# The end of a spectral ffn: the last back-transform with two places side by side in the two halves of the array

## The chip, the cores and the metric

The kernel runs on one core of a Trainium2 chip. The metric is the device time of one execution in microseconds, as the median of several runs. All data are fp32.

## What is computed

The reference is two layers on `x` of shape (2, 128, 64, 64). The first is a convolutional neighbourhood attention block, the second full attention over the 4096 tokens of each image, followed by a spectral ffn. Only the end of the ffn bears on the change:

```python
U_plus  = irfft(rfft(phi) * rfft(u))             # 16 filters, causal convolution over t
U_minus = sgn * irfft(rfft(phi) * rfft(u * sgn)) # the same with alternating signs
out = einsum('btkd,k,kde->bte', U_plus, s, Mpp) + einsum('btkd,k,kde->bte', U_minus, s, Mpm)
out = out + sum(shift(u, i) @ Mu[i] for i in range(3))
t = t + weighted sum of out over four branches (prefixes of 1, 1/2, 1/4 and 1/8 of the tokens)
x = from_tokens(t)                               # back to (2, 128, 64, 64)
```

The convolution is done by transforms of blocks of the tokens into a frequency domain of 160 bins (`BINS`), with real and imaginary parts as 320 rows (`NC`), products there, a projection from channels to channels in each bin, and a transform back, whose result is added to `t`.

## The kernel before

The kernel is one long program. In the last part, the tokens of an image lie in `xa[b]`, 128 channels by 4096 tokens, ordered by parity `par`, half `h`, block `f` (8 of them, `FB`) and place within a block `c`. Adding the transformed result there finishes the work; what then remains is to write the output.

The bins are handled in 40 groups of four (`GB`). A group consists of filter products (`group`, L1304, whose results ACT and DVE copy into `y` at L1305) and of the projection (`project`, L1316), 32 products that add up in one PSUM tile `acc`. ACT moves each `acc` into the tile `ob` (L1322), which holds channels by (parity, image, block, bin, real or imaginary part). The order of TensorE's work in this loop is written out by hand (`tc.manual_schedule`).

The back-transform takes the bins in three chunks: 0 to 63, 64 to 127 and 128 to 159, the last with 32 bins and so 64 rows only. For each image, parity and pair of blocks, `turn` brings the bins onto the partitions by transposes on TensorE (L1332), and ACT copies the result into `t` (L1334). `back` multiplies by the table `inv` (L1343). The first two chunks are woven into the loop as `back_into`, two blocks at a time, and DVE adds the result into `xa` (L1355). The table `inv` holds three parts of 128 rows; `_transforms` fills 320 of these rows, and the last 64 are zero.

The third chunk needs the last group and comes after the loop, in 16 rounds of four blocks:

```python
last = [(h, b, par, f0) for h in range(2) for b in range(NB) for par in range(2) for f0 in range(0, FB, 4)]
```

A round transposes four blocks one at a time, each to 64 rows (L1332), copies them (L1334), multiplies each by 128 columns of `inv` (L1343), and lets DVE add the result and `xa` into the output tile `o` (L1391). The transposes of a round are issued one round ahead. The same blocks are transposed twice, once for each half `h` of the tokens. After four rounds `o` is complete, and SP issues its transfer of 1 MB to the output (L1395). `o` has two buffers, `t` has two. PSUM has eight banks here: two for `acc`, and six in the pool `ps_c` with the tag `pc`, which `pc`, `pt` and `py` share in turn.

In the profile, L1332, L1334, L1343 and L1391 after 2207 us are this end.

Of the kernel before, what the change touches and what calls it, by code (L numbers as in the profile page):

```python
# [8 lines left out]
F32 = mybir.dt.float32  # L9
AF = mybir.ActivationFunctionType  # L10
ALU = mybir.AluOpType
# [3 lines left out]
P = 128  # L15
NB = 2
T = 4096
TH = T // 2
# [62 lines left out]
CB, FB, SG = 256, 8, 4  # L81
SB = CB // SG
NC = CB + SB

CHUNKS = (0, 1, 4, 5, 2, 3, 6, 7)
BINS = NC // 2
GB = 4
LG = 2 * FB
GROW = 4 * LG * KF


@with_exitstack
def kernel(
# [16 lines left out]
    nc = tc.nc  # L110
# [12 lines left out]
    xa = [xp.tile([P, T], F32, tag=f"xa{b}", name=f"xa{b}") for b in range(NB)]  # L123
# [15 lines left out]
    ident = const.tile([P, P], F32, name="ident")  # L139
# [79 lines left out]
    with l0a:  # L219
# [64 lines left out]
        for r in range(QT):  # L284
            lo = 6 - min(r, 6)
            src = bass.AP(
                rpb_pad.tensor, (RPR + r - 6) * RPW + 50, [[1, QT], [RPW, (HEADS - 1) * RPR - r // 7], [1, NTAB]]
            )
            rows_ = rev[r * QT : (r + 1) * QT].rearrange("p h n m -> p (h n) m")
# [483 lines left out]
        for k, (b, g) in enumerate(order):  # L773
            t = {}
# [499 lines left out]
    with ExitStack() as cv:  # L1274
        cp = cv.enter_context(tc.tile_pool(name="conv", bufs=5))
        obp = cv.enter_context(tc.tile_pool(name="ob", bufs=1))
        ps_c = cv.enter_context(tc.tile_pool(name="ps_c", bufs=6, space=PSUM))
        ps_p = cv.enter_context(tc.tile_pool(name="ps_p", bufs=2, space=PSUM))

        ob = obp.tile([P, 2, NB, FB, BINS, 2], F32, name="ob")  # L1280

        def inputs(q):

            ut = cp.tile([P, NB, 2, P], F32, tag="ut", name="ut")
            nc.sync.dma_start(
                out=ut.rearrange("p b s d -> p (b s d)"),
                in_=us[2 * q : 2 * q + 2].rearrange("g i r f b s d -> (g i r f) (b s d)"),
            )
            return ut

        def group():


            y = cp.tile([P, 8, KF, 2, 32], F32, tag="y", name="y", bufs=2)
            for q in range(GB // 2):
                ct, ut = ahead.pop(0)
                for par in range(2):

                    cv_ = ct[:, :, 0 : 288 + par * 32].rearrange("p o (l c) -> p o l c", l=2)[:, :, :, 0 : FB * KF]
                    for b in range(NB):  # L1300
                        for f in range(2):
                            fp = slice(f * 64, (f + 1) * 64)
                            pc = ps_c.tile([P, 2, 2, FB * KF], F32, tag="pc", name="pc")
                            nc.tensor.matmul(pc, lhsT=ut[fp, b, par, :], rhs=cv_[fp], start=True, stop=True)  # L1304
                            (nc.scalar.copy if f else nc.vector.tensor_copy)(  # L1305
                                y[:, 4 * f : 4 * f + 4, :, par, b * 2 * FB + q : (b + 1) * 2 * FB : 2],
                                pc.rearrange("p r l (t k) -> p (r l) k t", k=KF),
                            )
                if to_load:
                    q_ = to_load.pop(0)  # L1310
                    ahead.append((blocks(q_), inputs(q_)))
            return y

        def project(g, y, acc, l, k):

            nc.tensor.matmul(  # L1316
                acc, lhsT=(mmi if l else mpl)[:, k, :], rhs=y[:, 1::2, k, ::-1, :] if l else y[:, 0::2, k, :, :],
                start=(l == 0 and k == 0), stop=(l == 1 and k == KF - 1),
            )
            if l == 1 and k == KF - 1:  # L1320
                ov = ob.rearrange("p s b t g r -> p (s b t) (g r)")[:, :, g * GB * 2 : (g + 1) * GB * 2]
                nc.scalar.copy(  # L1322
                    ov.rearrange("p m (q x) -> p x m q", q=2), acc.rearrange("p (x m q) -> p x m q", x=4, q=2)
                )

        def turn(chunk, b, par, f0, n):

            bn = min(64, BINS - chunk * 64)
            pt = ps_c.tile([P, n, P], F32, tag="pc", name="pt")
            for j in range(n):  # L1330
                src = ob[:, par, b, FB - 1 - f0 - j, chunk * 64 : chunk * 64 + bn, :]
                nc.tensor.transpose(pt[0 : 2 * bn, j, :], src.rearrange("p g r -> p (g r)"), ident)  # L1332
            t = cp.tile([P, 4, P], F32, tag="t", name="t", bufs=2)
            nc.scalar.copy(t[0 : 2 * bn, 0:n, :], pt[0 : 2 * bn])  # L1334
            return t

        def back(chunk, t, n, h):

            bn = min(64, BINS - chunk * 64)
            c0, cn = (0, CB) if h is None else (h * P, P)  # L1340
            py = ps_c.tile([P, n, cn], F32, tag="pc", name="py")
            for j in range(n):
                nc.tensor.matmul(  # L1343
                    py[:, j, :], lhsT=t[0 : 2 * bn, j, :], rhs=inv[0 : 2 * bn, chunk, c0 : c0 + cn],
                    start=True, stop=True,
                )
            return py

        def back_into(chunk, b, par, f0):

            t = turn(chunk, b, par, f0, 2)
            yield True
            py = back(chunk, t, 2, None)
            xv = xa[b][:, par * TH : (par + 1) * TH].rearrange("p (h f c) -> p f h c", h=2, f=FB)[:, f0 : f0 + 2]
            nc.vector.tensor_tensor(xv, py.rearrange("p f (h c) -> p f h c", h=2), xv, ALU.add)  # L1355
            yield None

        places = [(b, par, f0) for b in range(NB) for par in range(2) for f0 in range(0, FB, 2)]
        to_load = list(range(BINS // 2))
        ahead = [(ct, inputs(to_load.pop(0))) for ct in first_blocks]  # L1360
        rest = []
        with tc.manual_schedule(engines={mybir.EngineType.PE}):
            y = group()
            for g in range(BINS // GB):
                following = group() if g + 1 < BINS // GB else None
                acc = ps_p.tile([P, 64 * GB], F32, tag="acc", name="acc")
                for l in range(2):
                    for k in range(KF):
                        project(g, y, acc, l, k)
                        if rest and k in ((3, 11) if g >= 128 // GB else (7,)):  # L1370
                            if next(rest[0], None) is None:
                                rest.pop(0)
                y = following
                if (g + 1) * GB in (64, 128):
                    rest += [back_into(g * GB // 64, *p) for p in places]
            for steps in rest:
                for _ in steps:
                    pass


        last = [(h, b, par, f0) for h in range(2) for b in range(NB) for par in range(2) for f0 in range(0, FB, 4)]
        ahead = [turn(2, *last[0][1:], 4)]
        for i, (h, b, par, f0) in enumerate(last):
            if i + 1 < len(last):
                ahead.append(turn(2, *last[i + 1][1:], 4))
            if par == 0 and f0 == 0:
                o = cp.tile([P, P, FB, 2], F32, tag="o", name="o", bufs=2)
            xv = xa[b][:, par * TH + h * (TH // 2) : par * TH + (h + 1) * (TH // 2)]
            xv = xv.rearrange("p (f c) -> p c f", f=FB)
            py = back(2, ahead.pop(0), 4, h)  # L1390
            nc.vector.tensor_tensor(  # L1391
                o[:, :, f0 : f0 + 4, par], py.rearrange("p f c -> p c f"), xv[:, :, f0 : f0 + 4], ALU.add
            )
            if par == 1 and f0 + 4 == FB:
                nc.sync.dma_start(out=outf[b, :, h * TH : (h + 1) * TH], in_=o.rearrange("p c f r -> p (c f r)"))  # L1395


# [19 lines left out]
def _transforms():  # L1417


    import numpy as np  # L1420

    f = np.arange(BINS)[None, :]
    real = (f == 0)

    def parts(n):
        n = np.arange(n)[:, None]
        a = 2 * np.pi * ((f * n) % NC) / NC
        return np.cos(a), -np.sin(a), (1.0 - 2.0 * (n % 2)) + 0.0 * f

    def pack(*cols):  # L1430
        return np.stack(cols, axis=-1).reshape(cols[0].shape[0], -1).astype(np.float32)

    c, m, alt = parts(CB)
    seg = pack(c, np.where(real, alt, m))
    filters = pack(c, np.where(real, 0.0, m), np.where(real, 0.0, -m), np.where(real, alt, c))
    back = np.zeros((3 * P, CB), np.float32)
    back[0:NC] = pack(np.where(real, 1.0, 2.0 * c) / NC, np.where(real, alt, 2.0 * m) / NC).T
    return seg, filters, back


# [49 lines left out]
```

## Time and profile before

| | |
|---|---|
| median of three runs | 2242.7 us (2241.91 to 2243.04) |
| the profiled execution | 2241.68 us |
| its span | 2240.0 us, 31648 instructions |
| TensorE (PE) busy | 2174.1 us, 97% |
| weight loads (PEld) busy | 1344.1 us, 60% |
| VectorE (DVE) busy | 940.5 us, 42% |
| ScalarE (ACT) busy | 780.6 us, 35% |
| GpSimd (POOL) busy | 276.2 us, 12% |
| granted TensorE clock, mean | 0.991 |

Times in the lines are from the start of the span. A line of groups names the source line, the engine, the operation, the written and read tiles, for TensorE its active rows and columns (`64*128`), the shape, and how often (x). Then come the busy time in us, the mean length of one in ns, and the idle time of the engine just before, with what ended it. In a timeline a line has the start, the length, the engine and the group, and in brackets the idle time before it. An fp32 product of TensorE leaves two records, a transpose one. Records of TensorE overlap, because one is still running out while the next streams in; the step from start to start is therefore shorter than the length of one.

### The profile page before, as it was taken

How to read it: one execution, taken by the hardware profiler on the slowest of the kernel's cores; microseconds unless marked ns; L12 is line 12 of the kernel's file. 1: busy time of each engine (PE TensorE's matmuls, PEld its weight loads, DVE VectorE, ACT ScalarE, POOL GpSimd, SP SyncE). 2: the span in 40 equal slices, each digit the busy share in tenths (PEclk: the TensorE clock that was granted, in tenths of full speed). 3: DMA queues.
4: the chain of work that ended last, by engine and by line, in shares of the span. 5: the costliest groups of instructions: out<-in, count | busy, mean ns of one | idle time of the engine just before them, and what ended most of it. 6: DMA issues, size and time to landing. Idle time of an engine off the chain costs nothing.

```text
span 2240.0 us, 31648 instructions
## 1 busy us (share of the span) xinstructions
PE 2174.1 (97%) x11888; PEld 1344.1 (60%) x11888; DVE 940.5 (42%) x3046; ACT 780.6 (35%) x1908; POOL 276.2 (12%) x353
## 2 busy tenths in 40 slices
PE   5899998999999999999999999999999999999998
PEld 3677765544454444544544447767677676767677
DVE  4799985434443346433333351222222323232323
ACT  2889883222332223222222332222322323232322
POOL 3377874200000000000000000000000000000000
PEclk8999998999999999999999999999999999999999
DMA  4222212011000016100000132212212122221101
GB/s 119 65 62 60 62 53 51 1 66 52 24 24 24 19 41 175 33 24 23 2 24 24 47 94 55 59 44 54 59 42 56 45 53 50 49 52 46 43 7 76
DMA packets 174810, 109.53 MB, mean 49 GB/s; under 512 B 26049, under 2 KB 159809, under 8 KB 174146
## 3 DMA queue, kind: packets, MB, share of 16 engines
q1 hardware_dynamic: 171818, 105.24, 18.0%
q10 hardware_dynamic: 2840, 2.27, 0.4%
q8 instruction: 94, 1.54, 0.3%
q14 instruction: 58, 0.48, 0.1%
HBM read 72.87 MB, written 34.60 MB: 48 GB/s over the span
## 4 chain that ended last, share of the span: by engine, by line
PE 86%; DVE 6%; POOL 3%; DMA 2%; ACT 1%; SPq 1%; issue 1%; DVEq 0%; ACTq 0%; POOLq 0%
PE acc L1316 25%; PE pc L1304 13%; PE bank L897 10%; PE own L925 10%; PE other L950 8%; PE bank L911 4%; PE py L1343 2%; PE bank L331 2%; PE bank L188 2%; PE bank L1042 2%; PE bank L1010 1%; PE bank L541 1%; DMA st<-in_m_minus_dram 1%; PE bank L505 1%; PE po L563 1%
## 5 line engine op out<-in xcount | busy, mean ns | idle before, releaser
L1305 DVE COPY y<-pc 128x512 f32<-128x512 f32 x320 | 221.4, 692 | 351.6 <-PE pc L1304 347.9
L904 ACT ACTIVATE e<-bank 128x512 f32<-128x512 f32 x288 | 171.8, 597 | 549.9 <-PE bank L897 415.2
L897 PE MATMUL bank<-cm 128*128 128x512 f32 x576 | 299.7, 605 | 1.4 <-DVE y L652 1.4
L1316 PE MATMUL acc<-y,mpl 128*128 128x256 f32 x1280 | 292.1, 382 | 0.0
L1316 PE MATMUL acc<-y,mmi 128*128 128x256 f32 x1280 | 288.0, 379 | 0.0
L1304 PE MATMUL pc<-ct,ut 64*128 64x512 f32 x1280 | 285.2, 595 | 0.9 <-issue 0.9
L1316 PEld LDWEIGHTS acc<-y,mpl 128*128 128x128 f32 x1280 | 238.2, 190 | 59.3 <-issue 29.6
L1316 PEld LDWEIGHTS acc<-y,mmi 128*128 128x128 f32 x1280 | 242.6, 190 | 32.6
L1305 ACT COPY y<-pc 128x512 f32<-128x512 f32 x320 | 204.5, 639 | 87.3 <-PE pc L1304 87.3
L925 PE MATMUL own<-et,tok 128*128 128x512 f32 x448 | 227.0, 593 | 1.9 <-DVE part L914 1.9
L950 PE MATMUL other<-e,tok 128*128 128x512 f32 x448 | 228.6, 592 | 0.0
L914 DVE CUSTOM_DVE_ANT_0 et<-bank,one 128x512 f32<-128x512 f32 x224 | 145.6, 687 | 166.0 <-PE bank L911 165.9
L1304 PEld LDWEIGHTS pc<-ct,ut 64*128 64x128 f32 x1280 | 121.5, 187 | 145.8 <-issue 140.6
L1322 ACT COPY ob<-acc 128x256 f32<-128x256 f32 x40 | 23.8, 595 | 431.2 <-PE acc L1316 431.2
L925 PEld LDWEIGHTS own<-et,tok 128*128 128x128 f32 x448 | 84.5, 190 | 109.8 <-issue 71.8
L950 PEld LDWEIGHTS other<-e,tok 128*128 128x128 f32 x448 | 85.1, 190 | 106.6 <-issue 105.7
L897 PEld LDWEIGHTS bank<-cm 128*128 128x128 f32 x576 | 96.2, 194 | 74.9 <-issue 46.1
L1355 DVE TENSOR_TENSOR xa<-py,xa 128x512 f32<-128x512 f32 x32 | 22.1, 691 | 281.4 <-PE py L1343 281.4
L911 PEld LDWEIGHTS bank<-ident,e 128*128 128x128 f32 x896 | 102.9, 141 | 56.5 <-issue 42.1
L160 POOL TENSOR_TENSOR ln_rs<-ln_rs,mhalf 128x4 f32<-128x4 f32 x24 | 24.3, 1011 | 848.0 <-DVE ln_rs L159 848.0
L528 ACT ACTIVATE p<-p,mn 128x196 f32<-128x196 f32 x256 | 114.4, 449 | 20.8 <-DVE mn L518 13.4
L911 PE MATMUL bank<-ident,e 128*128 128x128 f32 x896 | 117.3, 274 | 0.0
(199 smaller groups left out, 2311.1 us busy)
## 6 DMA issues: line engine op xcount, KB each, us to landing
ut<-us SPq DMA_DIRECT2D x80, 256.0 KB
us<-ub SPq DMA_DIRECT2D x64, 256.0 KB
vw<-vd SPq DMA_DIRECT2D x256, 49.0 KB
ct<-gs SPq DMA_DIRECT2D x160, 72.0 KB
ct<-gs SPq DMA_DIRECT2D x160, 64.0 KB
gs<-sum SPq DMA_DIRECT2D x20, 256.0 KB
vd<-v SPq DMA_DIRECT2D x128, 32.0 KB
st<-in_m_plus_dram SPq DMA_DIRECT2D x16, 256.0 KB
```

What stands on the lines that cost most here:

```text
L188: nc.tensor.transpose(ps[:, j * P : (j + 1) * P], src[:, j, :], ident)
L331: nc.tensor.matmul(pl, lhsT=wg[:, lo : lo + P], rhs=zT, start=True, stop=True)
L528: nc.scalar.activation(p, p, AF.Exp, bias=t[name + "mn"][:, h : h + 1], scale=-1.0, accum_out=t["den"][:, u, h : h + 1],)
L897: nc.tensor.matmul(ps, lhsT=cm[b][:, n * P : (n + 1) * P], rhs=cm[b][:, chunk(c)], start=True, stop=True)
L904: nc.scalar.activation(e, ps, AF.Exp, bias=0.0, scale=ASCALE, accum_out=part[:, n, c : c + 1])
L911: nc.tensor.transpose(pt[:, k * P : (k + 1) * P], es[k][:, m * P : (m + 1) * P], ident)
L914: nc.vector.tensor_tensor_reduce(et, pt, one, 1.0, 0.0, ALU.mult, ALU.add, part[:, n, a : a + 1])
L925: nc.tensor.matmul(own, lhsT=tok[b][:, n, :], rhs=e, start=first, stop=last)
L950: nc.tensor.matmul(other, lhsT=tok[b][:, 4 * CHUNKS[a] + j, :], rhs=es[j], start=(j == 0), stop=(j == 3))
L1304: nc.tensor.matmul(pc, lhsT=ut[fp, b, par, :], rhs=cv_[fp], start=True, stop=True)
L1305: (nc.scalar.copy if f else nc.vector.tensor_copy)(y[:, 4 * f : 4 * f + 4, :, par, b * 2 * FB + q : (b + 1) * 2 * FB : 2], pc.rearrange("p ...
L1316: nc.tensor.matmul(acc, lhsT=(mmi if l else mpl)[:, k, :], rhs=y[:, 1::2, k, ::-1, :] if l else y[:, 0::2, k, :, :], start=(l == 0 and k = ...
```

## The change

The last chunk gets a tile of its own, `ob_last`, in place of the end of `ob`. `turn` and `back` go; `back_into` holds their code for full chunks, and `t` has four buffers in place of two.

After the loop, 16 transposes take two neighbouring blocks at a time: 2 x 64 rows, the odd block on partitions 0 to 63 and the even one on 64 to 127. Each of the four combinations of image and parity has four of them in one PSUM bank, which ACT copies into `t`; these four tiles are kept for both halves `h`.

Then there are eight rounds, one for each half, image and parity. A round first multiplies the even blocks of `xa` by the identity into the bank `even`. Then come eight products of 64 rows, by turns from partitions 0 to 63 into the bank `odd` and from 64 to 127 onto `even`. ACT copies `even` to the even blocks of `o`, and DVE adds `odd` and `xa` into the odd ones. After two rounds the transfer of `o` is issued, as before. So that `inv` has the last bins on both halves of the partitions, its last 64 rows repeat the 64 before them.

```diff
+BC = 64
...
-        ob = obp.tile([P, 2, NB, FB, BINS, 2], F32, name="ob")
+        ob = obp.tile([P, 2, NB, FB, 2 * BC, 2], F32, name="ob")
+        ob_last = obp.tile([P, 2, NB, FB, BINS - 2 * BC, 2], F32, name="ob_last")
...
             if l == 1 and k == KF - 1:
-                ov = ob.rearrange("p s b t g r -> p (s b t) (g r)")[:, :, g * GB * 2 : (g + 1) * GB * 2]
+                o_, g0 = (ob, g * GB) if g * GB < 2 * BC else (ob_last, g * GB - 2 * BC)
+                ov = o_.rearrange("p s b t g r -> p (s b t) (g r)")[:, :, g0 * 2 : (g0 + GB) * 2]
...
         def back_into(chunk, b, par, f0):
 
-            t = turn(chunk, b, par, f0, 2)
+            pt = ps_c.tile([P, 2, P], F32, tag="pc", name="pt")
+            for j in range(2):
+                src = ob[:, par, b, FB - 1 - f0 - j, chunk * BC : (chunk + 1) * BC, :]
+                nc.tensor.transpose(pt[:, j, :], src.rearrange("p g r -> p (g r)"), ident)
+            t = cp.tile([P, 4, P], F32, tag="t", name="t", bufs=4)
+            nc.scalar.copy(t[:, 0:2, :], pt)
             yield True
-            py = back(chunk, t, 2, None)
+            py = ps_c.tile([P, 2, CB], F32, tag="pc", name="py")
+            for j in range(2):
+                nc.tensor.matmul(py[:, j, :], lhsT=t[:, j, :], rhs=inv[:, chunk, :], start=True, stop=True)
...
-        last = [(h, b, par, f0) for h in range(2) for b in range(NB) for par in range(2) for f0 in range(0, FB, 4)]
-        ahead = [turn(2, *last[0][1:], 4)]
-        for i, (h, b, par, f0) in enumerate(last):
-            if i + 1 < len(last):
-                ahead.append(turn(2, *last[i + 1][1:], 4))
-            if par == 0 and f0 == 0:
+        turned_ = {}
+        for b in range(NB):
+            for par in range(2):
+                pt = ps_c.tile([P, 4, P], F32, tag="pc", name="pt")
+                for i in range(4):
+                    src = ob_last[:, par, b, 2 * i : 2 * i + 2]
+                    nc.tensor.transpose(pt[:, 3 - i, :], src.rearrange("p m g r -> p (m g r)"), ident)
+                turned_[b, par] = cp.tile([P, 4, P], F32, tag="t", name="t", bufs=4)
+                nc.scalar.copy(turned_[b, par], pt)
+        for h in range(2):
+            for b in range(NB):
                 o = cp.tile([P, P, FB, 2], F32, tag="o", name="o", bufs=2)
-            xv = xa[b][:, par * TH + h * (TH // 2) : par * TH + (h + 1) * (TH // 2)]
-            xv = xv.rearrange("p (f c) -> p c f", f=FB)
-            py = back(2, ahead.pop(0), 4, h)
-            nc.vector.tensor_tensor(
-                o[:, :, f0 : f0 + 4, par], py.rearrange("p f c -> p c f"), xv[:, :, f0 : f0 + 4], ALU.add
-            )
-            if par == 1 and f0 + 4 == FB:
+                for par in range(2):
+                    xv = xa[b][:, par * TH + h * (TH // 2) : par * TH + (h + 1) * (TH // 2)]
+                    xv = xv.rearrange("p (f c) -> p f c", f=FB)
+                    odd, even = (ps_c.tile([P, 4, P], F32, tag="pc", name="py") for _ in range(2))
+                    nc.tensor.matmul(even, lhsT=ident, rhs=xv[:, 0::2], start=True, stop=False)
+                    for i in range(4):
+                        for q, py in ((0, odd), (1, even)):
+                            rows_ = slice(q * 64, (q + 1) * 64)
+                            nc.tensor.matmul(
+                                py[:, i, :], lhsT=turned_[b, par][rows_, i, :], rhs=inv[rows_, 2, h * P : (h + 1) * P],
+                                start=(q == 0), stop=(q == 0 or i == 3),
+                            )
+                    nc.scalar.copy(o[:, :, 0::2, par], even.rearrange("p f c -> p c f"))
+                    nc.vector.tensor_tensor(
+                        o[:, :, 1::2, par], odd.rearrange("p f c -> p c f"), xv[:, 1::2].rearrange("p f c -> p c f"), ALU.add
+                    )
                 nc.sync.dma_start(out=outf[b, :, h * TH : (h + 1) * TH], in_=o.rearrange("p c f r -> p (c f r)"))
...
     back[0:NC] = pack(np.where(real, 1.0, 2.0 * c) / NC, np.where(real, alt, 2.0 * m) / NC).T
+    back[NC:] = back[2 * P : NC]
```

More of the change, by code (lines that the diff above doesn't have):

```diff
@@ L1324, in project @@
                 )
[L1326 to L1345, printed above, removed]
-                )
-            return py
-        def back_into(chunk, b, par, f0):
-            t = turn(chunk, b, par, f0, 2)
+        def back_into(chunk, b, par, f0):
+            pt = ps_c.tile([P, 2, P], F32, tag="pc", name="pt")
[4 more added lines that the diff above has]
+            nc.scalar.copy(t[:, 0:2, :], pt)
             yield True
-            py = back(chunk, t, 2, None)
+            py = ps_c.tile([P, 2, CB], F32, tag="pc", name="py")
+            for j in range(2):
+                nc.tensor.matmul(py[:, j, :], lhsT=t[:, j, :], rhs=inv[:, chunk, :], start=True, stop=True)
             xv = xa[b][:, par * TH : (par + 1) * TH].rearrange("p (h f c) -> p f h c", h=2, f=FB)[:, f0 : f0 + 2]
@@ L1369 @@
                         project(g, y, acc, l, k)
-                        if rest and k in ((3, 11) if g >= 128 // GB else (7,)):
+                        if rest and k in ((3, 11) if g >= 2 * BC // GB else (7,)):
                             if next(rest[0], None) is None:
@@ L1373 @@
                 y = following
-                if (g + 1) * GB in (64, 128):
-                    rest += [back_into(g * GB // 64, *p) for p in places]
+                if (g + 1) * GB in (BC, 2 * BC):
+                    rest += [back_into(g * GB // BC, *p) for p in places]
             for steps in rest:
@@ L1378 @@
                     pass
-        last = [(h, b, par, f0) for h in range(2) for b in range(NB) for par in range(2) for f0 in range(0, FB, 4)]
-        ahead = [turn(2, *last[0][1:], 4)]
-        for i, (h, b, par, f0) in enumerate(last):
-            if i + 1 < len(last):
-                ahead.append(turn(2, *last[i + 1][1:], 4))
-            if par == 0 and f0 == 0:
-                o = cp.tile([P, P, FB, 2], F32, tag="o", name="o", bufs=2)
-            xv = xa[b][:, par * TH + h * (TH // 2) : par * TH + (h + 1) * (TH // 2)]
-            xv = xv.rearrange("p (f c) -> p c f", f=FB)
-            py = back(2, ahead.pop(0), 4, h)
-            nc.vector.tensor_tensor(
-                o[:, :, f0 : f0 + 4, par], py.rearrange("p f c -> p c f"), xv[:, :, f0 : f0 + 4], ALU.add
-            )
-            if par == 1 and f0 + 4 == FB:
+        turned_ = {}
```

## The prediction

> **What bounds the kernel now.** I read the page first: TensorE (PE) is busy in 97% of the span, and the chain of waits lies on it for 86%. Comparing the two programs engine by engine, every instruction up to the last eviction of the projection (L1322) stands in the same order in both. So only the stretch after that counts, from 2207.43 us to the end at 2240.0. Its groups by line and shape:
>
> ```profile
> L1343 PE MATMUL py<-inv,t 64*128 64x128 f32 x128 | 18.2, 284 | 0.3 <-ACT t L1334 0.3
> L1391 DVE TENSOR_TENSOR o<-py,xa 128x512 f32<-128x512 f32 x16 | 16.6, 1042 | 12.6 <-PE py L1343 12.6
> L1332 PE MATMUL pt<-ident,ob 128*64 128x128 f32 x64 | 9.8, 279 | 0.7 <-ACT ob L1322 0.7
> L1334 ACT COPY t<-pt 64x512 f32<-64x512 f32 x16 | 9.2, 578 | 16.0 <-PE pt L1332 16.0
> ```
>
> PE works 18.2 + 9.8 of some 26.4 us. VectorE (DVE) waits 12.6 us, all of it for PE, and ScalarE (ACT) waits 16.0 us for PE: both have room. The timeline shows the round that repeats 16 times, the start and the end:
>
> ```profile
> 2207.43 1.06 PE L1332 MATMUL pt<-ident,ob 128*64 128x128 f32 x8 [0.68 <-ACT ob L1322]
> ...
> 2211.51 0.63 PE L1332 MATMUL pt<-ident,ob 128*64 128x128 f32 x4
> 2211.61 1.04 DVE L1391 TENSOR_TENSOR o<-py,xa 128x512 f32<-128x512 f32 x1 [0.60 <-PE py L1343]
> 2212.07 0.96 PEld L1343 LDWEIGHTS py<-inv,t 64*128 64x128 f32 x8 [0.20 <-issue]
> 2212.07 1.16 PE L1343 MATMUL py<-inv,t 64*128 64x128 f32 x8
> ...
> 2213.26 1.04 DVE L1391 TENSOR_TENSOR o<-py,xa 128x512 f32<-128x512 f32 x1 [0.61 <-PE py L1343]
> ...
> 2231.77 2.05 PE L1343 MATMUL py<-inv,t 64*128 64x128 f32 x16
> 2232.97 1.98 DVE L1391 TENSOR_TENSOR o<-py,xa 128x512 f32<-128x512 f32 x2 [0.61 <-PE py L1343]
> ```
>
> Three prices follow. A round is 2213.26 - 2211.61 = 1.64 us. An fp32 product leaves two PE records; sixteen records take 2.05 and eight 1.16, so one record of 64 rows x 128 columns takes 0.89 / 8 = 0.111. Eight transposes take 1.06 and four 0.63: 0.108 each. Then 8 x 0.111 + 4 x 0.108 = 1.32 of the 1.64 is work, and 0.32 is the two changes of form in a round (128*64 to 64*128 and back).
>
> The place that tells what the other half of the array is worth is L1304, whose products of 64 rows alternate between rows 0 to 63 and 64 to 127. The timeline of its weight loads, and two rows of the page and its longer list:
>
> ```profile
> 2100.82 0.19 PEld L1304 LDWEIGHTS pc<-ct,ut 64*128 64x128 f32 x2 [0.24 <-issue]
> 2101.25 0.20 PEld L1304 LDWEIGHTS pc<-ct,ut 64*128 64x128 f32 x2 [0.23 <-issue]
> ```
> ```profile
> L1304 PE MATMUL pc<-ct,ut 64*128 64x512 f32 x1280 | 285.2, 595 | 0.9 <-issue 0.9
> L1042 PE MATMUL bank<-zc,mu 128*128 128x512 f32 x96 | 43.5, 594 | 0.0
> ```
>
> Two loads lie in one 0.19 us, and the next two follow 0.43 us later: records come in pairs. Busy time per record is 285.2 / 1280 = 0.223 at L1304 but 43.5 / 96 = 0.453 at L1042, which has as many columns and all 128 rows. The halves do run at once here.
>
> **What the Trainium skill says.** "TensorE: Matmul & The Clock Gate", Part 3 and the table under "Why this matters for your kernels": products in different row groups run concurrently, and a product of few rows alone takes as long as a full one. The trace agrees with both: 0.223 against 0.453, and 0.111 for 128 columns of 64 rows, a quarter of 0.43 to 0.45 for 512 columns. "TensorEngine Tiling (Array Packing)", Key Properties: changing the tiling mode, not just the tile, drains TensorE. The trace agrees: 0.32 a round for two changes, and L1304 pays none inside its run. The same page, Gotcha 1: different row tiles need different PSUM banks; the change gives each half its own (`odd`, `even`). "SBUF — State Buffer", Door 1: each access that crosses into a new 16-byte line pays. No row here shows a 16-byte step of a write.
>
> **The change part by part, on PE.**
> Removed: 16 rounds. From the first transpose to the end of the last record's streaming is 2207.43 to 2233.66 (last record begins at 2233.55, plus 0.111): 26.2 us.
> Added:
> (1) 16 transposes that fill all 128 rows of the result, two places each, in place of 64. All stand at the start, in the form of the projection before them: 16 x 0.108 = 1.7 us. Their stationary side has 128 columns in place of 64; L1332's own 128*128 records take 12.2 us of busy time for 64 among other work, and single ones start 0.11 apart. I take 0.108.
> (2) 8 identity products of 512 columns, which put `xa` of the even places into PSUM. Two records each; a 512-column record streams for 0.43 (the step of L1304): 0.86.
> (3) In each of the 8 new rounds, 8 products of 64 rows x 128 columns in alternating halves: 16 records in 8 pairs. If pairs run as at L1304, a pair takes 0.111: 0.89.
> (4) Two changes of form a round, 128 rows to 64 and back; the first round has one. Before, they cost 0.32 together. The single starts give 0.12 into the transposes, which load 64 columns, and 0.20 into the products, which load 128. Both new forms load 128 columns, and L1304 to L1316, the same passage, also loses 0.20 (last pair begins at 2104.26, streams to 2104.69, the next row works from 2104.89). So 0.40.
> A round: 0.86 + 0.89 + 0.40 = 2.15. All: 1.7 + 8 x 2.15 - 0.20 = 18.7 us. Gain: 26.2 - 18.7 = **7.5 us**.
>
> **What lies beside it.** ACT: 4 copies of 128x512 in place of 16 of 64x512. The first transposes' copy is needed only 0.86 us plus 12 transposes later, over 2 us, and takes about 0.6; the second is needed two us after that: hidden; uncovered, the first would cost its 0.6 once. The identity products read `xa`, last written by L1355 at 2205.06 + 0.69 us, before they start: no wait. Eight new ACT copies `o<-py` (0.64 by the strided copy of L1305) and 8 DVE adds in place of 16 (1.04 by L1391) run side by side, one of each in 2.15 us: hidden, except the last. Before, the last add began 0.38 us after the last record began and took 1.0; the same comes after, with the copy beside it: no change. Both write `o` in steps of 16 bytes, unseen in this trace: 0.7 us at the low end (L1355, unstrided), 2.0 us (twice L1391) at the high end; only the last eviction shows, -0.3 to +1.0 us. PSUM: the six `pc` banks hold four `pt` and one round, then three rounds; a bank comes back 6 us later, so no wait. Output: SP waits for DVE as before, now for ACT too. The last 1 MB still has 3.3 us to land:
>
> ```profile
> SPq L1486 <- DMA out_dram<-o: 3.3, 1, 3.3
> ```
>
> `o` has two buffers; the third write waits for the first transfer, issued after two rounds and landed about 3.9 us later (2234.97 to 2238.84 for the last one before); the third write comes three rounds, 6.4 us, after the issuing round's products: covered, unless rounds fall under some 1.7 us. Four transfers 4.3 us apart do not meet. Nothing else moves: POOL and the order of SP's queue are the same; `t` with four buffers and `ob` in two tiles alter no order, and I cost them at nothing because PE meets no wait at those lines before. The table `inv` gets 64 more filled rows in the same transfer: nothing.
>
> **Sum.** The profiled execution took 2241.68 us (span 2240.0): 2241.7 - 7.5 = 2234.2. The median of three runs is 1.0 higher, 2242.7, so **2235.2**. A measurement of this kernel can tell about 0.2%, 4.5 us, from no change.
>
> **The rivals.**
> A, pairs overlap (0.80): 2235.2. Ends: changes of form at 0.12 to 0.30 each (15 of them) -1.2 to +1.5; a pair at 0.107 to 0.13, -0.3 to +1.2; the last eviction -0.3 to +1.0. Own range 2233.4 to 2238.0.
> B, the halves do not overlap at this width (0.12): L1304 has 0.43 us of streaming under which a second load can hide; here it is 0.107, and loads of 128 columns in turn would set the pace. Then 16 records take 1.78: 0.89 more a round, 7.1 in all, gain 0.4: 2242.3, no change. For it: no 128-column alternation is in the trace. Against: the two loads of a pair begin together and each takes no longer (187 ns) than one alone at L1343 (187 ns).
> C, slower (0.05): one mechanism, in the eight products of a round. If every step to the other half drained the array like a change of form (0.16 on average) and nothing overlapped, a product would take 0.22 + 0.16 and the 64 of them 64 x (0.38 - 0.111) = 17.2 more than in A: 9.7 slower, 2252.4. It decides from 0.111 + 7.5 / 64 = 0.23 us a product on (0.30 for 0.2%). Against: L1304 alternates with no gap.
> D, evictions bind (0.03): if the 16-byte step costs over 2.15 us, DVE or ACT sets the round. At 2.6 us: the first starts at 2211.5, eight end at 2232.3 against 2234.95 now: 2240.0.
>
> **Numbers.** Faster by over 0.2%: nearly all of A, 0.80. Within 0.2%: B, D and a sliver of A, 0.15. Slower: C, 0.05. The range 2233.0 to 2240.1 holds A with its ends, and D; left out are B and C, 0.17.
>
> **What would show it.** After: L1332's successor with 16 transposes about 0.11 apart; weight loads of the 64-row products two at a time, a pair every 0.11; identity records 0.43 apart; DVE adds 2.15 us apart, DVE idle for PE between them; the last transfer issued near 2227.5. Loads in single file 0.11 apart would mean B; gaps between products, C; PE waiting for `o` evictions, D.

## The result, and the profile after

The changed kernel takes **2235.24 us** (median of eight runs, 2233.68 to 2237.13) against 2242.39 us before (eight runs beside it, 2240.02 to 2243.73). The ratio is 0.9972, with a 95% interval of 0.9963 to 0.9981: 7.15 us or 0.3% faster. The profiled execution took 2235.26 us, its span is 2233.6 us.

The groups of the end by line and shape, after:

```profile
L1389 PE MATMUL py<-inv,t 64*128 64x128 f32 x128 | 9.3, 285 | 0.0
L1385 PE MATMUL py<-xa,ident 128*128 128x512 f32 x16 | 8.9, 638 | 0.0
L1394 DVE TENSOR_TENSOR o<-py,xa 128x512 f32<-128x512 f32 x8 | 8.8, 1100 | 12.9 <-PE py L1389 12.9
L1393 ACT COPY o<-py 128x512 f32<-128x512 f32 x8 | 8.8, 1099 | 8.5 <-PE py L1389 8.5
L1375 PE MATMUL pt<-ident,ob_last 128*128 128x128 f32 x16 | 2.0, 276 | 0.7 <-ACT ob_last L1325 0.7
```

There are as many records of 64 rows as before, 128, with the same mean length (285 ns, 284 before). But they keep PE busy for 9.3 us in place of 18.2, so half of them run under the others. DVE and ACT still wait for PE only. The timeline of the same stretch:

```profile
2207.78 0.59 ACT L1325 COPY ob_last<-acc 128x256 f32<-128x256 f32 x1 [5.62 <-PE acc L1318]
2208.42 1.97 PE L1375 MATMUL pt<-ident,ob_last 128*128 128x128 f32 x16 [0.68 <-ACT ob_last L1325]
...
2212.37 1.10 DVE L1394 TENSOR_TENSOR o<-py,xa 128x512 f32<-128x512 f32 x1 [5.62 <-PE py L1389]
...
2213.32 1.16 PE L1389 MATMUL py<-inv,t 64*128 64x128 f32 x16
...
2214.41 1.12 PE L1385 MATMUL py<-xa,ident 128*128 128x512 f32 x2
2214.51 1.11 DVE L1394 TENSOR_TENSOR o<-py,xa 128x512 f32<-128x512 f32 x1 [1.04 <-PE py L1389]
...
2216.66 1.10 DVE L1394 TENSOR_TENSOR o<-py,xa 128x512 f32<-128x512 f32 x1 [1.03 <-PE py L1389]
...
2227.40 1.09 DVE L1394 TENSOR_TENSOR o<-py,xa 128x512 f32<-128x512 f32 x1 [1.00 <-PE py L1389]
```

Sixteen records now take 1.16 us, as long as eight took before. The adds start 2.15 us apart (2214.51 - 2212.37, 2216.66 - 2214.51), and each waits a good 1.0 us for PE.

The span alone hides part of the gain. The first line is the last copy of the projection, the point from which the kernels differ. It starts at 2207.78 here; before, the same copy stood 0.99 us earlier:

```profile
2206.79 0.59 ACT L1322 COPY ob<-acc 128x256 f32<-128x256 f32 x1 [5.62 <-PE acc L1316]
```

Up to it every engine runs the same operations in the same order in both. In the six profiles here that share the code of the change up to this copy, its start lies between 2205.78 and 2209.12: a spread of 3.3 us that no edit makes. So I measure the **tail**, from the start of this copy to the end of the span. Before: 2240.0 - 2206.79 = 33.2 us. After: 2233.6 - 2207.78 = 25.8 us. The gain in the tail is **7.4 us**. A tail comes from one profiled execution of each kernel, a median from several runs.

### The profile page after: what moved, and what is told of

Its sections match the earlier page's. It is cut to its first block, busy times and chain, and to the rows that moved or that the text cites. A ratio compares the mean times of both kernels' runs of the same rounds, so it can differ in the third digit from the quotient of the medians.

```text
span 2233.6 us, 31536 instructions
## 1 busy us (share of the span) xinstructions
PE 2165.4 (97%) x11856; PEld 1333.8 (60%) x11856; DVE 932.9 (42%) x3038; ACT 783.4 (35%) x1904; POOL 276.7 (12%) x353
## 4 chain that ended last, share of the span: by engine, by line
PE 86%; DVE 6%; POOL 3%; DMA 2%; ACT 1%; issue 1%; SPq 1%; ACTq 0%; POOLq 0%; DVEq 0%
PE acc L1318 25%; PE pc L1306 13%; PE bank L898 10%; PE own L926 10%; PE other L951 8%; PE bank L912 4%; PE bank L332 2%; PE bank L189 2%; PE bank L542 2%; PE bank L1011 1%; PE bank L1043 1%; PE py L1340 1%; DMA st<-in_m_minus_dram 1%; PE po L564 1%; PE bank L506 1%
## 5 line engine op out<-in xcount | busy, mean ns | idle before, releaser
L1325 ACT COPY ob<-acc 128x256 f32<-128x256 f32 x32 | 19.3, 604 | 387.0 <-PE acc L1318 387.0
L1342 DVE TENSOR_TENSOR xa<-py,xa 128x512 f32<-128x512 f32 x32 | 22.1, 692 | 281.4 <-PE py L1340 281.4
```

## The experiments

The question was which part brings the 7.4 us: the two halves at once, the 48 transposes fewer (with the changes of form that go with them), or the adds that the identity products take off DVE. The median before was 2243.48 us (20 runs) beside the first four experiments and 2243.17 us (9 runs) beside the others; a ratio is always against the kernel before.

### One half after the other

```diff
-                    for i in range(4):
-                        for q, py in ((0, odd), (1, even)):
+                    for q, py in ((0, odd), (1, even)):
+                        for i in range(4):
```

> The changed kernel with one edit: in each of the eight last rounds all four products of rows 0 to 63 come first and then all four of rows 64 to 127, so that the halves hardly meet. Instructions, loads and evictions are the same. Theory (the gain needs both halves at once): 16 records one after the other at 0.111 us are 1.78 in place of 0.89, so a round takes 3.04 in place of 2.15 us, 7.1 us in all but for the one pair that still meets; DVE adds 3.0 us apart; 2242.0 us, within 1 us of the kernel before. Rival (the gain is the halved transposes and their changes of form, and the halves' overlap adds nothing): the same time as the changed kernel, 2235, adds 2.15 apart.

Measured: 2239.21 us (16 runs), ratio 0.9983 (0.9975 to 0.9990); tail 2239.2 - 2209.12 = 30.1 us, 4.3 more than the change. The timeline:

```profile
2209.12 0.58 ACT L1325 COPY ob_last<-acc 128x256 f32<-128x256 f32 x1 [5.62 <-PE acc L1318]
...
2215.21 1.71 PE L1389 MATMUL py<-inv,t 64*128 64x128 f32 x16
2216.41 1.10 DVE L1394 TENSOR_TENSOR o<-py,xa 128x512 f32<-128x512 f32 x1 [1.60 <-PE py L1389]
...
2219.10 1.10 DVE L1394 TENSOR_TENSOR o<-py,xa 128x512 f32<-128x512 f32 x1 [1.60 <-PE py L1389]
```

A round is 2219.10 - 2216.41 = 2.69 us in place of 2.15, and all of the 0.55 lies in the 16 records (1.71 in place of 1.16). Alternation is therefore worth 4.3 us of this kernel. That is less than the 7 us expected: strictly in turn, the 16 records would take 2.05, as in the kernel before. The trace shows why. In one round (starts in us) the eight records of rows 0 to 63 start at 2212.519, and so on to 2213.179, 2213.290 and 2213.402. The first record of rows 64 to 127 starts at 2213.073, ahead of these last three, though it was issued after them. The records do not name their rows: the one at 2213.402 carries the signal that DVE's add waits for, so it ends rows 0 to 63. So PE ran work of the free half three records ahead of its place, and saved three steps of 0.11: 2.05 - 1.71 = 0.34.

### The transposes alone

```diff
-                    nc.tensor.matmul(even, lhsT=ident, rhs=xv[:, 0::2], start=True, stop=False)
-                    for i in range(4):
-                        for q, py in ((0, odd), (1, even)):
+                    for q, py in ((0, odd), (1, even)):
+                        for i in range(4):
...
-                    nc.scalar.copy(o[:, :, 0::2, par], even.rearrange("p f c -> p c f"))
...
+                    nc.vector.tensor_tensor(
+                        o[:, :, 0::2, par], even.rearrange("p f c -> p c f"), xv[:, 0::2].rearrange("p f c -> p c f"), ALU.add
+                    )
```

> The 16 full transposes of the change, but no identity product: DVE adds xa to both banks (16 adds, no ACT copy), and the products go one half after the other. PE then needs 1.78 us a round and no change of form, DVE 2 x 1.1 = 2.2. Theory (what the transposes save is most of what there was to save, and DVE is the next bound): adds follow each other every 1.1 us with no idle time, the last ends near 2229.4 in the changed kernel's trace against 2228.5 for the change; 2236.1 us, some 6 us under before. Rival (the halves at once and the identity carry the gain): DVE idle between adds, PE sets the pace, time at 2240 or more.

Measured: 2234.95 us (5 runs), ratio 0.9963 (0.9951 to 0.9976); tail 2234.0 - 2209.12 = 24.9 us. This is 0.9 us less than the change, with neither identity products nor halves by turns. In whole times the two cannot be told apart: the intervals of their ratios overlap. The timeline:

```profile
2212.84 1.10 DVE L1392 TENSOR_TENSOR o<-py,xa 128x512 f32<-128x512 f32 x1 [4.76 <-PE py L1388]
2213.82 1.10 DVE L1395 TENSOR_TENSOR o<-py,xa 128x512 f32<-128x512 f32 x1
2214.80 1.10 DVE L1392 TENSOR_TENSOR o<-py,xa 128x512 f32<-128x512 f32 x1
...
2216.89 12.44 SPq L1398 DMA_DIRECT2D out_dram<-o  x4
...
2221.20 1.09 DVE L1392 TENSOR_TENSOR o<-py,xa 128x512 f32<-128x512 f32 x1 [0.48 <-DMA out_dram<-o]
...
2227.89 1.08 DVE L1395 TENSOR_TENSOR o<-py,xa 128x512 f32<-128x512 f32 x1
```

DVE now sets the pace: no wait stands in the brackets but one. An add is 1.10 us long, yet the next starts 0.98 after it (2213.82 - 2212.84): queued adds overlap a little. I had expected 1.1. The one wait is for the first transfer, issued at 2216.89 and released some 4.3 us later; it costs 0.48 us.

This version saves more than transposes. All of them stand at the start, so its rounds have no change of form, where the kernel before had two in each of its 16 rounds. At the prediction's prices the transposes save 48 x 0.108 = 5.2 us of PE, and the changes of form 16 x 0.32 = 5.1. No run takes the two apart.

### The halves without the identity

The edit is that of the second experiment, but the loops stay as in the change (`for i`, then `for q`).

> As e2_transposes_alone, but the products alternate between the halves as in the change: PE needs 0.89 us a round, DVE still 2.2. Theory (DVE binds): the same as e2_transposes_alone within 0.5 us, about 2236; PE waits for PSUM banks. This says that the halves at once are worth something only where the adds are off DVE. Rival (PE's time counts whatever DVE does): some 7 us under e2_transposes_alone, about 2229.

Measured: 2234.24 us (5 runs), ratio 0.9964 (0.9951 to 0.9978); tail 2230.6 - 2205.78 = 24.8 us, as without alternation (24.9). The groups:

```profile
L1388 PE MATMUL py<-inv,t 64*128 64x128 f32 x128 | 11.3, 301 | 2.4 <-DVE o L1395 2.0 <-DVE o L1392 0.4
...
L1392 DVE TENSOR_TENSOR o<-py,xa 128x512 f32<-128x512 f32 x8 | 8.7, 1090 | 5.2 <-PE py L1388 4.8 <-DMA out_dram<-o 0.5
L1395 DVE TENSOR_TENSOR o<-py,xa 128x512 f32<-128x512 f32 x8 | 8.6, 1081 | 0.0
```

PE waits for DVE to free banks (2.0 + 0.4 us). Overlapping the halves buys nothing once 16 adds stand on DVE, and the rival, which gave it 7 us by itself, falls. The halves are worth 4.3 us in the change only because the identity products there hold DVE at one add a round, and those cost PE 0.86 us a round plus two changes of form.

### Two rounds together

```diff
+        evens = [seeded(0)]
         turned_ = {}
...
+        evens.append(seeded(1))
+        for r, (h, b, par) in enumerate(order_):
...
+                if r:
+                    evens += [seeded(r), seeded(r + 1)]
```

`seeded(r)` issues the identity product of round r. The identity products of two rounds stand together, the first one ahead of the transposes; the `even` banks come by turns from the pools of `acc` and `pc`.

> The change with the identity products of two rounds one after the other and then the sixteen products of both, so 7 changes of form in place of 15, and with the first identity product ahead of the transposes, where PE waits for ACT's last copy of the projection. Theory (a change of form costs 0.2 us each, and the wait of 0.65 us before the first transpose is free time): 8 x 0.2 + 0.65 = 2.25 us less than the change, about 2233.0; adds 0.9 and 3.0 us apart by turns, 3.9 for two. Rival (the changes of form are hidden, or the third output tile waits for its transfer): no gain, 2235 or more, with waits of ACT and DVE for the transfer.

Measured: 2232.51 us (5 runs), ratio 0.9953 (0.9940 to 0.9965); tail 2230.8 - 2207.33 = 23.5 us, 2.3 less than the change (2.25 expected). The timeline:

```profile
2207.13 1.02 PE L1381 MATMUL py<-xa,ident 128*128 128x512 f32 x2
2207.33 0.59 ACT L1325 COPY ob_last<-acc 128x256 f32<-128x256 f32 x1 [5.62 <-PE acc L1318]
2207.98 1.96 PE L1391 MATMUL pt<-ident,ob_last 128*128 128x128 f32 x16
...
2211.92 2.09 DVE L1410 TENSOR_TENSOR o<-py,xa 128x512 f32<-128x512 f32 x2 [5.63 <-PE py L1405]
...
2215.82 2.10 DVE L1410 TENSOR_TENSOR o<-py,xa 128x512 f32<-128x512 f32 x2 [1.81 <-PE py L1405]
```

Two rounds take 2215.82 - 2211.92 = 3.90 us in place of 2 x 2.147 = 4.29. The difference of 0.39 is the two changes of form that fell away: 0.20 each, the price used in the prediction. The first transpose still starts 0.65 us after the copy does (0.64 in the change), so the early identity product cost no time: it ran while PE waits for that copy.

### Unstrided writes of `o`

```diff
+                    flat = o.rearrange("p c f r -> p (c f r)").rearrange("p (k c f) -> p k c f", k=4, f=4)
-                    nc.scalar.copy(o[:, :, 0::2, par], even.rearrange("p f c -> p c f"))
+                    nc.scalar.copy(flat[:, 2 * par], even.rearrange("p f c -> p c f"))
...
-                        o[:, :, 1::2, par], odd.rearrange("p f c -> p c f"), xv[:, 1::2].rearrange("p f c -> p c f"), ALU.add
+                        flat[:, 2 * par + 1], odd.rearrange("p f c -> p c f"), xv[:, 1::2].rearrange("p f c -> p c f"), ALU.add
```

> The change, but ACT and DVE write o without steps, so the output's elements stand in another order; the reads of PSUM and of xa keep their steps. In the change both take 1.10 us where I had taken 0.64 for ACT. Theory (the writes in steps of 16 bytes cost it): ACT 0.6 us, DVE 0.7 to 1.04. Rival (the reads across a PSUM bank in steps of 512 bytes cost it): both stay at 1.1. Only the last eviction lies on the path: at most 0.5 us less in all.

The output's elements then stand in another order, so this version does not compute the result and only prices the writes. Measured in one run: 2235.89 us; tail 2234.2 - 2208.48 = 25.7 us, against 25.8. The groups:

```profile
L1395 DVE TENSOR_TENSOR o<-py,xa 128x512 f32<-128x512 f32 x8 | 8.3, 1042 | 13.3 <-PE py L1389 13.3
...
L1394 ACT COPY o<-py 128x512 f32<-128x512 f32 x8 | 4.7, 585 | 12.1 <-PE py L1389 12.1
```

The copy falls from 1099 to 585 ns, the add from 1100 to 1042. The step of the writes costs ACT half a microsecond and DVE 0.06. Hardly any of it is in the time, since PE sets the round and the last add ends almost as late: 20.65 us after the last copy of the projection began (2228.10 + 1.03 - 2208.48), in the change 20.71.

### The identity in half of the rounds

```diff
-                    nc.tensor.matmul(even, lhsT=ident, rhs=xv[:, 0::2], start=True, stop=False)
+            if r == 4:
+                evens[4], evens[6] = seeded(4), seeded(6)
...
+            if par == 0:
+                nc.scalar.copy(o[:, :, 0::2, par], even.rearrange("p f c -> p c f"))
+            for f, py in ((1, odd), (0, even))[: 1 + par]:
+                nc.vector.tensor_tensor(
+                    o[:, :, f::2, par], py.rearrange("p f c -> p c f"), xv[:, f::2].rearrange("p f c -> p c f"), ALU.add
+                )
```

Rounds of `par` 0 run as in the change; those of `par` 1 have no identity product and give both banks to DVE. The first identity product stands ahead of the transposes, as in the fourth experiment, and `o` has four tiles, in the space of a `y` that is no longer used.

> A version between the change and e3_halves_no_identity: alternating halves, identity and ACT for the even blocks of four rounds of eight (first one ahead of the transposes, then one, then two together), DVE for the other twelve banks, and four output tiles (in a free y buffer). PE needs about 12.2 us from the transposes on, DVE 12 x 0.97. Theory (each engine's time adds up as measured so far): from the start of the last copy of the projection to the first add 4.6, adds 11.6, the last transfer 3.9 and the close 1.2: 21.3 us to the end of the span, against 25.8 for the change and 24.8 for e3; 4.5 us under the change, 3.5 under e3, some 2231. Rival (transfers 2.9 us apart of 1 MB each bind, or PSUM banks run out): 23 us or more.

Measured: 2230.88 us (5 runs), ratio 0.9951 (0.9939 to 0.9964); tail 2228.8 - 2206.95 = 21.9 us (21.3 expected), 4 less than the change. The timeline of DVE and SP:

```profile
2211.60 11.83 DVE L1413 TENSOR_TENSOR o<-py,xa 128x512 f32<-128x512 f32 x12 [5.68 <-PE py L1406]
...
2214.74 9.08 SPq L1417 DMA_DIRECT2D out_dram<-o  x4
```

Twelve adds run in 11.83 us without a gap. Here PE is made lighter until DVE is full. The tail counts up: 4.65 to the first add, 11.83 of adds, 5.4 from there to the end.

The rival was close. The packets of the four transfers run without a break from 2215.59 to 2227.28, 11.7 us for 4 MB, and keep the 16 DMA engines 87% busy; in the change they take 15.5 us with pauses, at 66%. From the start of the last issue (2223.49) to the end of the span 5.3 us pass, where the change needs 5.0: half of the 0.6 us by which the tail missed the expectation. So DVE is full here and the output transfers nearly so; a lighter DVE alone would probably gain little more, though no run tries it.

### Four output tiles

The third experiment, with four tiles of `o` in place of two by turns:

```diff
-                o = cp.tile([P, P, FB, 2], F32, tag="o", name="o", bufs=2)
+                o = o4[:, 2 * h + b]
```

> e3_halves_no_identity with four output tiles in place of two, so that no write waits for a transfer. Theory (the 0.48 us that DVE waited for the first transfer lies on the path): 24.3 us from the last copy of the projection to the end of the span, 0.5 less than e3. Rival (something else is late at that place): the same 24.8.

Measured: 2233.07 us (5 runs), ratio 0.9960 (0.9948 to 0.9973); tail 2232.7 - 2208.34 = 24.4 us, against 24.8 with two tiles. The groups:

```profile
L1393 DVE TENSOR_TENSOR o<-py,xa 128x512 f32<-128x512 f32 x8 | 8.7, 1085 | 4.8 <-PE py L1389 4.8
L1396 DVE TENSOR_TENSOR o<-py,xa 128x512 f32<-128x512 f32 x8 | 8.5, 1067 | 0.0
```

The 0.5 us that DVE waited for the transfer is gone from the row, and 0.4 of it from the tail. In whole times the two cannot be told apart.

### The last tile in two transfers

The sixth experiment, with the last two adds split by columns, and half of the last tile sent after each half:

```diff
+            pieces = ((0, 64), (64, P)) if r == 7 else ((0, P),)
+            for lo, hi in pieces:
```

> e6_identity_in_half with the last two adds split by columns, and the last output tile sent in two transfers of 0.5 MB. Theory (of the 3.9 us that the last transfer takes to land, half of what is above the fixed part goes, and the first half leaves 1.1 us earlier): 1.0 us less than e6, 20.3 us from the last copy of the projection to the end of the span. Rival (the transfer's fixed part, or the two halves one behind the other, eat it): the same as e6 or more.

Measured: 2230.74 us (5 runs), ratio 0.9947 (0.9934 to 0.9961); tail 2230.6 - 2208.53 = 22.1 us, no gain over 21.9. The timeline of SP:

```profile
2216.32 9.14 SPq L1420 DMA_DIRECT2D out_dram<-o  x5
```

The last issue ends at 2216.32 + 9.14 = 2225.46, and the span 5.1 us later; in the sixth experiment it was 2228.8 - 2223.82 = 5.0 us for twice the bytes. The second half lands no sooner than a whole tile, as the rival had it. The packets show why. The second half is issued at 2225.13, but its packets start at about 2226.9, when those of the first half end: 1.8 us later, against 0.8 in the change (2228.56 to 2229.38). The first half waited likewise, 1.4 us (2224.16 to 2225.58), for the third tile. As in the sixth experiment the packets run without a break, from 2217.16 to 2228.93: 11.8 us for the same 4 MB.

The sixth and eighth experiments are the fastest versions of the study: some 12 us under the kernel before and 4 us of tail under the change.

## Why the prediction was right

**The sum.** Predicted: 18.7 us on PE from the first transpose to the end of the last record's streaming, gain 7.5. Measured: 2208.42 to about 2227.2, 18.8 us; gain 7.4 in the tail, 7.15 in the medians. That the median of 2235.24 lies on the 2235.2 of the prediction to 0.1 us is luck: the runs spread over some 3.5 us, and the median before was 0.3 lower in this comparison than the 2242.7 from which it subtracted.

**(1) The transposes**: 16 in 1.97 us with the last one's run-out, 0.109 apart (0.108 taken). The 128 columns of their stationary side cost nothing more.

**(2) to (4), the round**: 2.147 us against 2.15. The products' records start in pairs 7 ns apart (2211.387 and 2211.394), a pair every 0.111. An identity record is followed by the next after 0.43, plus 0.10 if it is the first. A change of form is a gap of 0.09 and this 0.10 of a longer first step (the first pair has it too: 0.21 to the next in place of 0.11), 0.19 in all; the two-round experiment confirms the 0.20 taken. What decided was to take the price of the pair from L1304, at four times the columns, and to trust it at 128. No line of the trace before showed it there; it was a bet, with a chance of 0.80 put on it, and it held. The Trainium skill, "TensorE: Matmul & The Clock Gate", Part 3, says that loads of another row group are pulled ahead of running products; the 1.16 us for 16 records agree. The same part says that the products themselves keep their order of start. The first experiment differs: a record of the other half started ahead of three issued earlier (2213.073 against 2213.179 and later), and the measurement decides.

**Two readings** of the prediction were loose and cost nothing. "18.2 + 9.8 of some 26.4 us" adds to 28.0: the last record of each group runs out under the next group, so busy times of groups cannot be summed to a share. And 2104.89 is not where L1316 starts: its first record starts at 2104.78 in the trace, and the difference of 0.1 is its longer first step.

**What lies beside it.** Two terms were mis-sized and cost nothing. The copy `o<-py` takes 1.10 us, not 0.64: the L1305 copy was the wrong row, and the unstrided version shows that the 16-byte step makes the difference (0.585). The add takes 1.10, not 1.04. Both lay within the bounds given, 0.7 to 2.0. At the end of the kernel, from the end of the last record's streaming (2227.2) to the end of the last evictions (2228.5), there are 1.3 us, as before (2233.66 to 2234.95): "no change" was right, since copy and add end together.

**The output.** The third write of `o` was covered in the change, as predicted: due one round after the add at 2218.81, at 2220.96 and so 5.3 us after the first issue (2215.69), it starts at 2221.01. But the margin was smaller than I wrote. In the second experiment the transfer releases DVE 4.3 us after its issue, not 3.9, and rounds of 1.95 us met it, although I had put the point at 1.7.

**The rivals.** B (no overlap at 128 columns) fell by the 1.16 us; C (a drain at each change of half) too, and the grouped order, which has fewer such changes, was slower and not faster. D needed evictions over 2.15 us; they take 1.10.

**What the prediction did not see** is that the halves at once and the identity products were not needed for the gain. Its rival B put all but 0.4 of the 7.5 us on the halves at once. In its own prices, the halves save 7.1 us (128 x 0.111 - 8 x 0.89), but the identity products cost 8 x 0.86 = 6.9 and their changes of form 3.0: more than the halves bring. The rest of the sum, transposes and the old changes of form, is 5.2 + 5.1. The experiments agree: fewer transposes, held for both `h`, and no changes of form are enough for 8.3 us of tail by themselves. Identity and halves together move work from DVE to PE and ACT, and at one identity product in every round PE ends up a little slower (2.15 us a round) than DVE would be with two adds (1.95). Of the versions run, the best lies between, with the identity in every other round.

## What to carry to other kernels

Price a step that moves work from one engine to another from both engines: here each gave about 2 us a round, so the all-or-nothing versions lie within 1 us of each other and a split wins. Put instructions of one form together, as each change of form cost 0.20 us of PE here, and put independent work into a wait that exists anyway. Where the code ahead of a change shifts by microseconds from run to run, compare the part that differs, from a common instruction to the end.

## What the runs showed of the hardware that I had not expected

- ACT's copy pays for a write in steps of 16 bytes (1.10 against 0.585 us for 512 elements a partition), DVE's add hardly (1.10 against 1.042). That is 0.51 / 512, or 1.0 ns an element, on ACT.
- Adds of DVE that stand ready in its queue start 0.98 us apart while each is 1.10 long. A stretch full of these adds is 0.1 us an add shorter than the lengths say.
- PE takes products of the free half of the rows ahead of their turn, here by three records: grouped order loses 0.55 us in a round where full serialization would lose 0.89.
- In the change and in the first, fourth and fifth experiments, ACT's first copy into a reused `o` starts 0.32 us after its wait has ended; its other copies need no such time. In the first experiment the transfer was issued 7 us before, so it is hardly the transfer; the cause stays open, and PE's rounds absorb it.
